# A four-layer transformer with a routed expert stage: first expert weights and output bias fetched per block, first product computed turned, gates moved to the final sum

## The chip, the cores and the metric

The kernel runs on one core of one Trainium2 chip. The metric is the device time of one execution in microseconds (us). Two executions are spoken of: the timed runs, of which there are 14, and one profiled execution, which left the trace. All durations of single instructions come from the trace.

The engines are PE (matrix products), DVE and POOL (elementwise work; POOL also issues the scatters), ACT (activation functions, which also issues some transfers) and SP, which here only issues transfers. Every engine executes its own instructions in program order.

## The reference, cut to what matters

A batch of 64 x 64 tokens of width 128 passes an attention layer with relative positions (L0), a self/cross attention layer with a feed-forward part (L1), a gating layer (L2), and a last layer (L3): self attention, cross attention and a mixture of 8 experts, of which each token uses 2. Only the last step is touched:

```
h      = layer_norm(x)
logits = h @ rw.T + rb
vals, idx = top_k(logits, 2);  gates = softmax(vals)
h1 = gelu(h @ fc1_w[e].T + fc1_b[e])          # 128 -> 512, for expert e
eo = h1 @ fc2_w[e].T + fc2_b[e]               # 512 -> 128
out = x + gates[0] * eo[idx 0] + gates[1] * eo[idx 1]
```

## The kernel before, in words

The 4096 tokens are worked on in 8 groups of 512 (4 blocks of 128 tokens, `NBLK`). The first layer has its order written out by hand. For the other layers the Python generators of `drive` (line 149) put out the instructions of several groups alternately, and a scheduler orders each engine's instructions at build time by its own model; `experts` (line 649) is the "fill" that `drive` steps on between the others. Nearly all instructions carry line 74, that of a helper, so groups are told apart by tile names.

**Routing** (`router`, line 1279, once for each group). It takes the two best experts and their gates, counts the rows of each expert with small products (`pr`), and scatters each normalised token twice, to the places of its two experts, into a table in device memory (`hrows`, POOL, 8 scatters per group). Each row carries 4 more columns: token number, first expert, and two gate values (lines 1345 to 1347). Then lines 1367 to 1379 build the matrix of gates, turn it on PE (`pgt`), copy it (DVE, `T<-pgt`), multiply it with the output biases of all experts (`tok<-fc2b`) and add the result to `x`.

**Tables** (`table`, line 657). When all groups of a part are routed (5 groups in the first part, 3 in the second, `PARTS`), DVE computes for each block of 128 rows its place in `hrows` and its expert. There are 47 and 31 blocks (`NSLOT`), 78 in all.

**Blocks** (the loop of line 822). In step t the program puts out, in this order: `load(t+6)`, `first(t)`, `hidden_turned(t-1)`, `second(t-3)`, `turn(t+2)`.

- `load` (710): SP reads the block's place out of the table into a register (`value`, a TENSOR_LOAD at line 311), computes the address, and issues the transfer of 128 rows into one of 8 places (`rin`, in the trace under the name `km`).
- `turn` (719): PE turns the rows (`xt`), ACT scales them and adds the shift (`vp`); DVE computes where each result row goes (`tob`) and its gate (`m`) in four small instructions.
- `first` (744): PE reads the expert's place into a register and multiplies: 128 tokens by 512 hidden columns, one product `f<-fcw,vp` with the tokens as stationary operand. `fcw` holds both weights of all 8 experts on chip (1024 columns for each). DVE copies the 512 columns out (`h`).
- `hidden_turned` (753): four PE transposes (`ht`), then four Gelu instructions on ACT, with the bias of the first product as per-partition scalar.
- `second` (768): four products that add up into 128 tokens by 128 columns; DVE multiplies by the gate on the way out (`y`, in the trace `km<-f,m`), and POOL scatters the result (`yrows`).

In the trace each of these fp32 products stands as two MATMUL records, a transpose as one.

**Sums** (`read` 789, `summed` 804). When all results of a part are scattered, the two result rows of each token are read back (one transfer on SP's queue, one on ACT's), POOL adds `x` and the first, DVE adds the second, and SP writes the output. For the 5 groups of the first part this goes on between the blocks of the second part; the last 3 groups are summed at the end.

The 8 transfers of first weights are issued with the 8 of second weights in `load_expert` (1409), long before the experts start.

Of the kernel before, what the change touches and what calls it, by code (L numbers as in the profile page):

```python
# [16 lines left out]
P = 128  # L17
# [16 lines left out]
ROWW = D + 4  # L34
NEG = -1.0e30
EPS = 1e-5

# [57 lines left out]
def kernel(ctx: ExitStack, tc: tile.TileContext, a: dict, out: bass.AP):  # L95
# [553 lines left out]
    def experts():  # L649
# [7 lines left out]
        def table(h):  # L657
# [11 lines left out]
            for e in range(1, NE):  # L669
# [13 lines left out]
            nc.vector.scalar_tensor_tensor(rb, eb, float(REGION), jb, op0=ALU.mult, op1=ALU.add)  # L683

            nc.vector.tensor_scalar(rb, rb, float(NE * REGION), float(P), ALU.min, ALU.mult)
            tab = wtile([1, 2, ns], f"table{h}", 1, I32)
            nc.vector.tensor_copy(tab[:, 0, :], rb[0:1, :])
            nc.vector.tensor_scalar(
                tab[:, 1, :], eb[0:1, :], float(NE - 1), 1024.0, ALU.min, ALU.mult
            )  # L690

            hot = wtile([NE, ns], "hotb", 1)
            nc.vector.tensor_scalar(hot, eb[0:NE, :], lane[0:NE, :], None, ALU.is_equal)
# [12 lines left out]
        def slot(i):  # L706
            h = sum(i >= LAST[k] for k in range(NH))
            return h, i - (LAST[h] - NSLOT[h])

        def load(i):  # L710
            h, j = slot(i)
            rows_in = rin[i % 8]
            at = value(nc.sync, tables[h][0][0:1, 0, j : j + 1], NE * REGION * P)
            ld = nc.sync.dma_start(rows_in, hrows[h][bass.ds(at, P), :])
            for sc in done["scatters"][h]:
                tc.add_manual_dep(ld.ins, sc.name, LANDED, reason="all rows are in place")
            held[i] = {"in": rows_in}

        def turn(i):
            h, j = slot(i)  # L720
            b = held[i]
            rows_in = b["in"]
            pt = pmm("xt")
            nc.tensor.transpose(pt[:, 0:P], rows_in[:, 0:D], ident)
            b["x"] = wtile([P, P], "vp", 3)
            nc.scalar.activation(b["x"], pt[:, 0:P], AF.Identity, scale=col("moe_g"), bias=col("moe_b"))

            m = wtile([P, 3], "m", 12)
            b["to"] = wtile([P, 1], "tob", 16, U32)
            nc.vector.tensor_tensor(  # L730
                m[:, 0:1], rows_in[:, D + 1 : D + 2], tables[h][1][:, j : j + 1], ALU.is_equal
            )
            nc.vector.tensor_tensor(
                m[:, 2:3], rows_in[:, D + 1 : D + 2], tables[h][1][:, j : j + 1], ALU.not_equal
            )
            nc.vector.tensor_scalar(
                b["to"], m[:, 2:3], float(PARTS[h] * T), rows_in[:, D : D + 1], ALU.mult, ALU.add
            )
            nc.vector.tensor_scalar(
                m[:, 1:2], m[:, 0:1], rows_in[:, D + 3 : D + 4], rows_in[:, D + 2 : D + 3], ALU.mult, ALU.add  # L740
            )
            b["gate"] = m[:, 1:2]

        def first(i):
            h, j = slot(i)
            b = held[i]
            b["e"] = value(nc.tensor, tables[h][0][0:1, 1, j : j + 1], (NE - 1) * 1024)
            ps = pmm("f1")
            nc.tensor.matmul(ps, lhsT=b["x"], rhs=fcw[:, bass.ds(b["e"], 512)], start=True, stop=True)
            b["u"] = wtile([P, 512], "h1", 4)  # L750
            nc.vector.tensor_copy(b["u"], ps)

        def hidden_turned(i):
            h, j = slot(i)
            b = held[i]
            pt = pmm("ht")
            for c in range(NFC):
                nc.tensor.transpose(pt[:, c * P : (c + 1) * P], b["u"][:, c * P : (c + 1) * P], ident)
            b["h"] = wtile([P, 512], "s", 10)
            for c in range(NFC):  # L760
                nc.scalar.activation(
                    b["h"][:, c * P : (c + 1) * P], pt[:, c * P : (c + 1) * P], AF.Gelu,
                    bias=tables[h][2][:, c, j : j + 1],
                )

# [2 lines left out]
        def second(i):  # L768
            h, j = slot(i)
            b = held.pop(i)  # L770
            po = pmm("f2")
            for c in range(NFC):
                nc.tensor.matmul(
                    po[:, 0:D], lhsT=b["h"][:, c * P : (c + 1) * P],
                    rhs=fcw[:, bass.ds(b["e"] + (512 + c * D), D)],
                    start=(c == 0), stop=(c == NFC - 1),
                )
# [44 lines left out]
        for t in range(-6, total + 3):  # L822
            h = sum(t + 6 >= at for at in LAST)
            while h < NH and done["routed"] < sum(PARTS[: h + 1]):
                yield
            if h < NH and h not in tables:
                yield from table(h)
            if t + 6 < total:
                load(t + 6)
            if 0 <= t < total:  # L830
                first(t)
            if 0 <= t - 1 < total:
                hidden_turned(t - 1)
            if 0 <= t - 3 < total:
                second(t - 3)
            if 0 <= t + 2 < total:
                turn(t + 2)

            for h in range(NH - 1):
                gl, at = divmod(t - 3 - LAST[h] - 4, 4)  # L840
# [15 lines left out]
    def other_layers(ends):  # L856
# [4 lines left out]
        fc2b = wtile([NE, D], "fc2b", 1)  # L861
# [4 lines left out]
        nc.scalar.dma_start(fc2b, a["fc2b"])  # L866

        bkm = wtile([P, 2, 4], "bkm", 1)
        for i, name in enumerate(("sa_in_b", "ca_in_b")):
# [409 lines left out]
        def router(g, hT, x, zx):  # L1279
# [59 lines left out]
            nc.vector.tensor_tensor(e2, e2, g1, ALU.mult)  # L1339
# [6 lines left out]
            nc.vector.tensor_copy(meta(2), e2)  # L1346
            nc.vector.tensor_tensor(meta(3), g1, e2, ALU.subtract)
            for n in range(2):
                if g < NG - 1:
                    yield  # L1350
# [14 lines left out]
            yield  # L1365

            gates = wtile([P, NBLK, NE], "gates", 3)
            nc.vector.tensor_tensor(gates, hots[0], last(g1[:, :], NE), ALU.mult)
            nc.vector.tensor_tensor(hots[1], hots[1], last(e2[:, :], NE), ALU.mult)
            nc.vector.tensor_tensor(gates, gates, hots[1], ALU.add)  # L1370
            yield
            pgt = extra("pgt")
            for k in range(NBLK):
                nc.tensor.transpose(pgt[0:NE, k * P : (k + 1) * P], gates[:, k, :], ident)
            gT = wtile([NE, T], "T", 4)
            nc.vector.tensor_copy(gT, pgt[0:NE, :])
            yield
# [26 lines left out]
        return pools["mid"].tile(shape, dtype, tag=name, name=name)  # L1404


    fcw = mtile([P, NE * 1024], "fcw")

    def load_expert(e):
        nc.scalar.dma_start(fcw[:, e * 1024 : e * 1024 + 512], a["fc1"][e])  # L1410
        nc.scalar.dma_start(
            v3(fcw[:, e * 1024 + 512 : (e + 1) * 1024], NFC), a["fc2"][e].rearrange("(f c) d -> c f d", c=P)
        )

    start = mtile([P, NE], "start")
# [85 lines left out]
```

## Time and profile before

| | us |
|---|---|
| median of the 14 timed runs (lowest to highest) | 1761.66 (1756.85 to 1767.45) |
| the profiled execution's own time | 1758.07 |
| its span in the trace | 1756.3 |
| busy: PE / DVE / ACT / POOL | 1614.6 / 1214.0 / 992.6 / 914.0 |
| first row load issued by SP | 1520.9 |
| last result scatter issued by POOL | 1740.4 |

How to read it: times in windows count from the start of the span. The slices on the page cut the span into 40 equal parts, one digit each, in tenths. In a group's or tile's line come engine, operation, operands (result, then sources), count, and duration in nanoseconds as least/median/most. Engine names with a q (SPq) are an engine's own queue of issuing and register instructions, which are not counted as busy. An arrow in square brackets says how long an engine was idle before and what ended that. The clock (PEclk) is the share of full speed that PE was granted.

### The profile page before, as it was taken

How to read it: one execution, taken by the hardware profiler on the slowest of the kernel's cores; microseconds unless marked ns; L12 is line 12 of the kernel's file. 1: busy time of each engine (PE TensorE's matmuls, PEld its weight loads, DVE VectorE, ACT ScalarE, POOL GpSimd, SP SyncE). 2: the span in 40 equal slices, each digit the busy share in tenths (PEclk: the TensorE clock that was granted, in tenths of full speed). 3: DMA queues.
4: the chain of work that ended last, by engine and by line, in shares of the span. 5: the costliest groups of instructions: out<-in, count | busy, mean ns of one | idle time of the engine just before them, and what ended most of it. 6: DMA issues, size and time to landing. Idle time of an engine off the chain costs nothing.

```text
span 1756.3 us, 46242 instructions
## 1 busy us (share of the span) xinstructions
PE 1614.6 (92%) x18026; PEld 1165.2 (66%) x18026; DVE 1214.0 (69%) x3289; ACT 992.6 (57%) x2712; POOL 914.0 (52%) x875
## 2 busy tenths in 40 slices
PE   7799999999999999699998999899888988679996
PEld 5566666666666666477676776667666767557774
DVE  4577676767676767578877786777566874556663
ACT  4456464646464645255655556666677853236663
POOL 3445464646473737567766666534222243554454
PEclk9999999999999999899999999999889987589998
DMA  6664554555455545410000000000000000112143
GB/s 175 157 162 137 134 140 130 140 130 140 129 139 132 139 140 152 150 37 8 11 26 28 26 15 13 13 2 2 8 14 14 2 21 20 55 51 57 54 122 90
DMA packets 215160, 136.78 MB, mean 78 GB/s; under 512 B 38896, under 2 KB 198786, under 8 KB 214816
## 3 DMA queue, kind: packets, MB, share of 16 engines
q1 hardware_dynamic: 186880, 90.54, 20.6%
q10 hardware_dynamic: 23520, 34.75, 6.1%
q0 software_dynamic: 4544, 8.54, 1.4%
q8 instruction: 144, 2.36, 0.6%
q14 instruction: 72, 0.59, 0.1%
HBM read 66.51 MB, written 68.19 MB: 77 GB/s over the span
## 4 chain that ended last, share of the span: by engine, by line
PE 64%; DVE 16%; ACT 8%; POOL 5%; issue 3%; DMA 3%; another core or an unknown queue 1%; POOLq 0%; SPq 0%; ACTq 0%; DVEq 0%
PE av L74 8%; PE psv L74 8%; PE proj L74 7%; PE pt L74 6%; PE psk L74 6%; PE f L74 6%; PE tok L74 5%; PE pbd L74 4%; PE psc L74 3%; DVE mx L74 3%; DVE s L74 3%; PE acc L74 3%; PE sc L74 3%; ACT z L74 3%; PE tr L74 2%
## 5 line engine op out<-in xcount | busy, mean ns | idle before, releaser
L74 ACT ACTIVATE s<-s,nm 128x128 f32<-128x128 f32 x512 | 198.0, 388 | 245.4 <-DVE nm L74 221.6
L74 POOL TENSOR_TENSOR s<-s,sm 128x512 f32<-128x512 f32 x128 | 130.6, 1042 | 257.1 <-DVE sm L74 257.1
L74 PE MATMUL pt<-ident,s 128*128 128x128 f32 x1536 | 213.4, 282 | 21.4 <-ACT kT L74 7.8
L74 POOL TENSOR_TENSOR s<-s,mx 128x512 f32<-128x512 f32 x160 | 164.1, 1046 | 110.9 <-DVE mx L74 110.7
L74 PEld LDWEIGHTS pt<-ident,s 128*128 128x128 f32 x1536 | 176.5, 145 | 42.3 <-issue 15.7
L74 ACT ACTIVATE pT<-pt 128x512 f32<-128x512 f32 x256 | 142.0, 606 | 83.0 <-PE pt L74 72.1
L74 POOL TENSOR_TENSOR rs<-rs,nhalf 128x4 f32<-128x4 f32 x80 | 81.6, 1021 | 189.6 <-DVE rs L74 157.3
L74 POOL TENSOR_TENSOR skew<-skew,mb 128x512 f32<-128x512 f32 x128 | 160.1, 1273 | 29.9 <-DMA skew<-scr 29.3
L74 PEld LDWEIGHTS av<-vb,pT 128*64 128x64 f32 x4096 | 133.0, 143 | 21.0 <-issue 16.3
L74 PE MATMUL av<-vb,pT 128*64 128x18 f32 x4096 | 141.3, 216 | 4.7 <-issue 2.5
L74 DVE TENSOR_REDUCE mx<-s 128x8 f32<-128x512 f32 x160 | 102.8, 674 | 44.2 <-ACT s L74 44.2
L74 POOL DMA_INDIRECT yrows<-km,tob x78 | 76.3, 979 | 99.2 <-DVE m L74 71.1
L74 PE MATMUL psv<-wv,kv 128*128 128x256 f32 x512 | 127.4, 392 | 0.0
L74 PE MATMUL psk<-kv,wk 128*128 128x512 f32 x256 | 127.0, 618 | 0.0
L74 PE MATMUL sc<-km,qs 32*64 32x256 f32 x2048 | 106.0, 425 | 19.6 <-ACT qs L74 13.9
L74 DVE COPY pT<-pt 128x512 f32<-128x512 f32 x128 | 82.1, 682 | 37.5 <-PE pt L74 37.5
L74 PEld LDWEIGHTS psv<-wv,kv 128*128 128x128 f32 x512 | 92.2, 189 | 15.1 <-issue 1.0
L74 PEld LDWEIGHTS av<-pT,v 128*64 128x64 f32 x2048 | 66.5, 138 | 52.8 <-issue 31.1
L74 PEld LDWEIGHTS pbd<-rT,qp 64*128 64x128 f32 x1024 | 62.1, 187 | 57.4 <-DVE qp L74 55.7
L74 DVE TENSOR_TENSOR s<-sc,mb 128x512 f32<-128x512 f32 x128 | 81.8, 680 | 26.0 <-PE sc L74 25.9
L74 DVE TENSOR_TENSOR s<-psc,skew 128x512 f32<-128x512 f32 x128 | 87.4, 683 | 13.6 <-issue 7.3
L74 ACT ACTIVATE z<-z,nmr,rs 128x128 f32<-128x128 f32 x160 | 66.2, 492 | 53.3 <-DVE nmr L74 39.5
(237 smaller groups left out, 3746.5 us busy)
## 6 DMA issues: line engine op xcount, KB each, us to landing
scr<-stage SPq DMA_DIRECT2D x64, 516.0 KB
skew<-scr SPq DMA_DIRECT2D x128, 256.0 KB
hrows<-pad ACTq DMA_DIRECT2D x66, 330.0 KB
ctx<-in_ctxT SPq DMA_DIRECT2D x24, 256.0 KB
km<-hrows SPq DMA_DIRECT2D x78, 66.0 KB
fcw<-in_fc ACTq DMA_DIRECT2D x16, 256.0 KB
kv<-in_xT SPq DMA_DIRECT2D x8, 256.0 KB
kv<-in_ctxT SPq DMA_DIRECT2D x8, 256.0 KB
```

What stands on the lines that cost most here:

```text
L74: ins = it(*args, **kw)
```

## The change

1. `fcw` keeps only the second weights. In `load`, SP reads a second table value (the expert), and issues two more transfers for each block: the first weights (128 x 512, 256 KB) into a ring of 6 (`w1s`) and the output bias of the expert, repeated to all 128 partitions (64 KB), into a ring of 8 (`b2s`). `load_expert` issues 8 transfers instead of 16.
2. `first` makes the product turned: four products, each with 128 columns of the weights as stationary operand and the block's 128 tokens streaming. The result has hidden columns on partitions, and Gelu reads it straight from PSUM; the copy `h` and the four transposes are gone, and `second` follows two steps after `first` instead of three.
3. `second` adds the bias on the way out instead of multiplying by the gate. The table `gate` keeps the two gates of each token on chip, and `summed` applies them: eight DVE instructions of 128 x 128 for each group, none on POOL.
4. The gate columns of the rows (528 to 520 bytes) and the gate computation in `turn` (four instructions to two) go, and so does the part of `router` that multiplies gates by biases.
5. In a step the program now puts out `first(t)`, `second(t-2)`, `load(t+6)`, `turn(t+2)`.

```diff
@@ table
-            tab = wtile([1, 2, ns], f"table{h}", 1, I32)
+            tab = wtile([1, 3, ns], f"table{h}", 1, I32)
...
+            nc.vector.tensor_scalar(tab[:, 2, :], eb[0:1, :], float(NE - 1), None, ALU.min)
@@ load
+            w, bias = w1s[i % 6], b2s[i % 8]
+            e = value(nc.sync, tables[h][0][0:1, 2, j : j + 1], NE - 1)
+            nc.sync.dma_start(w, a["fc1"][bass.ds(e, 1), :, :].rearrange("o p f -> (o p) f"))
+            nc.sync.dma_start(bias, a["fc2b"][bass.ds(e, 1), :].to_broadcast([P, D]))
@@ first
-            nc.tensor.matmul(ps, lhsT=b["x"], rhs=fcw[:, bass.ds(b["e"], 512)], start=True, stop=True)
-            b["u"] = wtile([P, 512], "h1", 4)
-            nc.vector.tensor_copy(b["u"], ps)
-        def hidden_turned(i):
...
-                nc.tensor.transpose(pt[:, c * P : (c + 1) * P], b["u"][:, c * P : (c + 1) * P], ident)
+                nc.tensor.matmul(
+                    ps[:, c * P : (c + 1) * P], lhsT=b["w"][:, c * P : (c + 1) * P], rhs=b["x"],
+                    start=True, stop=True,
+                )
@@ second
-            nc.vector.tensor_scalar(y, po[:, 0:D], b["gate"], None, ALU.mult)
+            nc.vector.tensor_tensor(y, po[:, 0:D], b["bias"], ALU.add)
@@ summed
-            nc.gpsimd.tensor_tensor(o, ys[0], v3(xs[g][:, :], NBLK), ALU.add)
-            nc.vector.tensor_tensor(o, o, ys[1], ALU.add)
+            for k in range(NBLK):
+                nc.vector.scalar_tensor_tensor(
+                    o[:, k, :], ys[0][:, k, :], gate[:, g, 0, k : k + 1], x3[:, k, :], op0=ALU.mult, op1=ALU.add
+                )
+                nc.vector.scalar_tensor_tensor(
+                    o[:, k, :], ys[1][:, k, :], gate[:, g, 1, k : k + 1], o[:, k, :], op0=ALU.mult, op1=ALU.add
+                )
@@ the loop of steps
-            if t + 6 < total:
-                load(t + 6)
             if 0 <= t < total:
                 first(t)
-            if 0 <= t - 1 < total:
-                hidden_turned(t - 1)
-            if 0 <= t - 3 < total:
-                second(t - 3)
+            if 0 <= t - 2 < total:
+                second(t - 2)
+            if t + 6 < total:
+                load(t + 6)
@@ router, at the end
-            gates = wtile([P, NBLK, NE], "gates", 3)
...
-            pb = tokens_by(lambda c: gT, lambda c: fc2b)
-            nc.vector.tensor_tensor(x, pb, x, ALU.add)
@@ load_expert
-        nc.scalar.dma_start(fcw[:, e * 1024 : e * 1024 + 512], a["fc1"][e])
```

More of the change, by code (lines that the diff above doesn't have):

```diff
@@ L33 @@
 LAST = [sum(NSLOT[: h + 1]) for h in range(NH)]
-ROWW = D + 4
+ROWW = D + 2
 NEG = -1.0e30
@@ L685, in table @@
             nc.vector.tensor_scalar(rb, rb, float(NE * REGION), float(P), ALU.min, ALU.mult)
-            tab = wtile([1, 2, ns], f"table{h}", 1, I32)
+            tab = wtile([1, 3, ns], f"table{h}", 1, I32)
             nc.vector.tensor_copy(tab[:, 0, :], rb[0:1, :])
             nc.vector.tensor_scalar(
-                tab[:, 1, :], eb[0:1, :], float(NE - 1), 1024.0, ALU.min, ALU.mult
+                tab[:, 1, :], eb[0:1, :], float(NE - 1), 512.0, ALU.min, ALU.mult
             )
+            nc.vector.tensor_scalar(tab[:, 2, :], eb[0:1, :], float(NE - 1), None, ALU.min)
             hot = wtile([NE, ns], "hotb", 1)
@@ L716, in load @@
                 tc.add_manual_dep(ld.ins, sc.name, LANDED, reason="all rows are in place")
-            held[i] = {"in": rows_in}
+            w, bias = w1s[i % 6], b2s[i % 8]
+            e = value(nc.sync, tables[h][0][0:1, 2, j : j + 1], NE - 1)
+            nc.sync.dma_start(w, a["fc1"][bass.ds(e, 1), :, :].rearrange("o p f -> (o p) f"))
+            nc.sync.dma_start(bias, a["fc2b"][bass.ds(e, 1), :].to_broadcast([P, D]))
+            held[i] = {"in": rows_in, "w": w, "bias": bias}
         def turn(i):
@@ L726, in turn @@
             nc.scalar.activation(b["x"], pt[:, 0:P], AF.Identity, scale=col("moe_g"), bias=col("moe_b"))
-            m = wtile([P, 3], "m", 12)
+            m = wtile([P, 1], "m", 12)
             b["to"] = wtile([P, 1], "tob", 16, U32)
-            nc.vector.tensor_tensor(
-                m[:, 0:1], rows_in[:, D + 1 : D + 2], tables[h][1][:, j : j + 1], ALU.is_equal
-            )
[L733 to L742, printed above, removed]
+            nc.vector.tensor_scalar(
+                m, rows_in[:, D + 1 : D + 2], tables[h][1][:, j : j + 1], float(PARTS[h] * T),
+                ALU.not_equal, ALU.mult,
+            )
+            nc.vector.tensor_tensor(b["to"], m, rows_in[:, D : D + 1], ALU.add)
         def first(i):
@@ L746, in first @@
             b = held[i]
-            b["e"] = value(nc.tensor, tables[h][0][0:1, 1, j : j + 1], (NE - 1) * 1024)
+            b["e"] = value(nc.tensor, tables[h][0][0:1, 1, j : j + 1], (NE - 1) * 512)
             ps = pmm("f1")
-            nc.tensor.matmul(ps, lhsT=b["x"], rhs=fcw[:, bass.ds(b["e"], 512)], start=True, stop=True)
-            b["u"] = wtile([P, 512], "h1", 4)
-            nc.vector.tensor_copy(b["u"], ps)
-        def hidden_turned(i):
-            h, j = slot(i)
-            b = held[i]
-            pt = pmm("ht")
             for c in range(NFC):
-                nc.tensor.transpose(pt[:, c * P : (c + 1) * P], b["u"][:, c * P : (c + 1) * P], ident)
+                nc.tensor.matmul(
+                    ps[:, c * P : (c + 1) * P], lhsT=b["w"][:, c * P : (c + 1) * P], rhs=b["x"],
+                    start=True, stop=True,
+                )
             b["h"] = wtile([P, 512], "s", 10)
@@ L761, in hidden_turned @@
                 nc.scalar.activation(
-                    b["h"][:, c * P : (c + 1) * P], pt[:, c * P : (c + 1) * P], AF.Gelu,
+                    b["h"][:, c * P : (c + 1) * P], ps[:, c * P : (c + 1) * P], AF.Gelu,
                     bias=tables[h][2][:, c, j : j + 1],
@@ L774, in second @@
                     po[:, 0:D], lhsT=b["h"][:, c * P : (c + 1) * P],
-                    rhs=fcw[:, bass.ds(b["e"] + (512 + c * D), D)],
+                    rhs=fcw[:, bass.ds(b["e"] + c * D, D)],
                     start=(c == 0), stop=(c == NFC - 1),
@@ L806, in summed @@
             o = wtile([P, NBLK, D], "o", 2)
-            nc.gpsimd.tensor_tensor(o, ys[0], v3(xs[g][:, :], NBLK), ALU.add)
-            nc.vector.tensor_tensor(o, o, ys[1], ALU.add)
+            x3 = v3(xs[g][:, :], NBLK)
+            for k in range(NBLK):
[5 more added lines that the diff above has]
+                )
             nc.sync.dma_start(out[g * NBLK : (g + 1) * NBLK].rearrange("k p d -> p k d"), o)
@@ L821, in experts @@
         reads = {}
-        for t in range(-6, total + 3):
+        for t in range(-6, total + 2):
             h = sum(t + 6 >= at for at in LAST)
@@ L827, in experts @@
                 yield from table(h)
+            if 0 <= t < total:
+                first(t)
+            if 0 <= t - 2 < total:
+                second(t - 2)
             if t + 6 < total:
                 load(t + 6)
-            if 0 <= t < total:
-                first(t)
-            if 0 <= t - 1 < total:
-                hidden_turned(t - 1)
-            if 0 <= t - 3 < total:
-                second(t - 3)
             if 0 <= t + 2 < total:
@@ L839, in experts @@
             for h in range(NH - 1):
-                gl, at = divmod(t - 3 - LAST[h] - 4, 4)
+                gl, at = divmod(t - 2 - LAST[h] - 4, 4)
                 if 0 <= gl < PARTS[h]:
@@ L860, in other_layers @@
         rw = wtile([P, NE], "rw", 1)
-        fc2b = wtile([NE, D], "fc2b", 1)
         nc.scalar.dma_start(w2l, a["w2l"])
@@ L865, in other_layers @@
         nc.scalar.dma_start(rw, a["rw"])
-        nc.scalar.dma_start(fc2b, a["fc2b"])
         bkm = wtile([P, 2, 4], "bkm", 1)
@@ L1338, in router @@
             nc.vector.reciprocal(g1, g1)
-            nc.vector.tensor_tensor(e2, e2, g1, ALU.mult)
+            nc.vector.tensor_copy(gate[:, g, 0, :], g1)
+            nc.vector.tensor_tensor(gate[:, g, 1, :], e2, g1, ALU.mult)
             def meta(c):
@@ L1345, in router @@
             nc.vector.tensor_copy(meta(0), tok[:, PLACE[g][1] * NBLK : (PLACE[g][1] + 1) * NBLK])
-            nc.vector.tensor_copy(meta(2), e2)
-            nc.vector.tensor_tensor(meta(3), g1, e2, ALU.subtract)
             for n in range(2):
@@ L1364, in router @@
             done["routed"] += 1
-            yield
-            gates = wtile([P, NBLK, NE], "gates", 3)
[L1368 to L1377, printed above, removed]
-            pb = tokens_by(lambda c: gT, lambda c: fc2b)
-            nc.vector.tensor_tensor(x, pb, x, ALU.add)
         fb = cols[:, _C["fc1_b"][0] : _C["fc1_b"][1]].rearrange("p (e c) -> p c e", c=NFC)
@@ L1404, in mtile @@
         return pools["mid"].tile(shape, dtype, tag=name, name=name)
-    fcw = mtile([P, NE * 1024], "fcw")
+    fcw = mtile([P, NE * 512], "fcw")
+    w1s = [mtile([P, 512], f"w1s{i}") for i in range(6)]
+    b2s = [mtile([P, D], f"b2s{i}") for i in range(8)]
+    gate = mtile([P, NG, 2, NBLK], "gate")
     def load_expert(e):
-        nc.scalar.dma_start(fcw[:, e * 1024 : e * 1024 + 512], a["fc1"][e])
         nc.scalar.dma_start(
-            v3(fcw[:, e * 1024 + 512 : (e + 1) * 1024], NFC), a["fc2"][e].rearrange("(f c) d -> c f d", c=P)
+            v3(fcw[:, e * 512 : (e + 1) * 512], NFC), a["fc2"][e].rearrange("(f c) d -> c f d", c=P)
         )
```

## The prediction, as put on record before the run

> **What bounds the kernel now.** I read the page's slices first, then the busy times by window, then PE's timeline inside a window, then SP's queue there. The page:
>
> ```profile
> span 1756.3 us, 46242 instructions
> PE   7799999999999999699998999899888988679996
> PEclk9999999999999999899999999999889987589998
> ```
>
> (PEclk is the clock that PE was granted.) Everything that the change touches lies in the last eighth, apart from the loads of the weights near 730 us. The windows there (window, its length, busy PE, PEld, DVE, ACT, POOL with counts, clock, DMA share, GB/s):
>
> ```profile
> 1500.00:1550.00 50.00, 33.42 (x143) 23.58 (x142) 27.40 (x187) 11.40 (x31) 28.62 (x30) 0.64 0.20 59
> 1577.00:1681.00 104.00, 104.00 (x680) 80.22 (x679) 71.66 (x264) 66.23 (x219) 42.39 (x44) 1.00 0.24 65
> ```
>
> Until 1575 no engine is full: the last groups' routing, POOL's scatters and the first blocks wait for each other. From 1577 PE is busy all of 104 us and nothing else is. One period of PE's timeline (start, length, operation):
>
> ```profile
> 1657.84 0.27 PE L74 MATMUL xt<-ident,km 128*128 128x128 f32 x1
> 1657.95 1.02 PE L74 MATMUL f<-fcw,vp 128*128 x2
> 1658.81 0.60 PE L74 MATMUL ht<-ident,h 128*128 128x128 f32 x4
> 1659.25 1.06 PE L74 MATMUL f<-fcw,s 128*128 x8
> 1660.14 0.27 PE L74 MATMUL xt<-ident,km 128*128 128x128 f32 x1
> ```
>
> Lengths overlap; starts count. One block: xt 0.11, first product 0.86, transposes 0.44, second product 0.89, together 2.30 us. The second product shows the price of a record with 128 streaming columns and its own weights: 0.89/8 = 0.111.
>
> SP is the queue that the change loads. Five row loads that ran nearly unhindered, their register loads, and SP's waits in the stretch from 1576 to 1680 (total, times, longest):
>
> ```profile
> L74 SPq DMA_DIRECT2D km<-hrows x5: 332/332/333, 1529.9 to 1533.4; - x5
> L311 SPq TENSOR_LOAD <-table x5: 267/268/272, 1530.2 to 1533.8; - x5
> SPq L74 <- PE xt L74: 57.9, 43, 2.8
> ```
>
> Five issues lie 3.5 us apart from first to last: 3.5/4 = 0.88 us for each load, of which 0.33 is the transfer's issue, 0.27 the register load, 0.28 address, semaphores and gaps. In the full stretch SP waited 57.9 of 104 us, so 46.1/45 blocks = 1.02 us at most went to a load.
>
> **The change, part by part.**
>
> *PE, per block.* The product turned is 4 x 2 records of 128 columns: 8 x 0.111 = 0.89 in place of 0.86. The transposes' 0.44 go. New sum 0.11 + 0.89 + 0.89 = **1.89**, 0.41 less. The first product's weights now change with each record, but so they do in `f<-fcw,s`, whose cadence I used.
>
> *DVE, ACT, POOL, per block.* DVE loses the copy `h` (0.69) and two of four small instructions; adding the bias costs what the gate's product did (0.35). ACT keeps four Gelu and `vp`: 66.23 us in 45 blocks, 1.47 each. POOL keeps one scatter per block, at 1.27 when back to back. None reaches 1.89; this gains nothing by itself.
>
> *SP, per block.* Before: one load, 0.88. After: rows 0.88, weights with their own register load 0.88, bias without one, 0.88 - 0.27 - 0.05 = 0.56. Sum **2.32 us**, more than PE's 1.89 and level with the old 2.30. The issue itself depends little on size (ctx, 256 KB in rows of 2 KB: median 328 ns; rows: 332). Bounds: 2.2 if semaphore waits share a slot; 2 x 1.02 + 0.70 = 2.74 if the full stretch's 1.02 is all work. I take 2.32, since the five loads had the fewest waits in them.
>
> A rule speaks against the change here. The Trainium skill, "DMA: Bandwidth & Descriptors", section "Latency and other measured facts", puts a floor of about 600 ns under a tensor_load. The rows here show 268. By the page a block would cost SP 2 x 0.33 more, 2.98 us, and the sum below would end some 50 us later; the measured row decides.
>
> *Waits added.* The weights' transfer waits for `first` six blocks back, the bias for DVE's add eight back. Behind them in SP's queue stand the next rows, read-backs and output writes; PE's `xt` waits for the rows. With SP slowest these waits are over before SP arrives.
>
> *Data.* 320 KB more per block. In the crowded window 727 to 750 the engines moved 231 GB/s; in the full stretch they are 24% busy at 65 GB/s. At 2.32 us per block the addition is 138 GB/s, total about 200: carried, with latency. Lower bound 0; upper bound, if issues slow to the 445 ns of fcw's loads in that crowd, 3 x 0.11 = 0.33 per block. That end lies inside the 2.74.
>
> *Sums.* POOL's add (1.26) and DVE's (0.69) become eight DVE instructions. No such row exists; a 128 x 512 add takes 0.69, so a quarter with its fixed part about 0.22; a 128 x 128 `z` on chip took 0.16 to 0.35. I take 0.28, 2.2 per group. SP's output write waits for it: read-back issued, 3 us to land, 2.2 to sum, against 4.6 us of SP's other work in between: about 1 us lost, five times; plus ten issues of 0.45. Together **9** (4 to 15).
>
> *Routing.* Eight groups lose 4 `pgt`, 8 `tok<-fc2b`, a copy and an add. Mostly they fill waits, but at the start of the experts two are on the path: DVE, with the table half made, waits for such a product,
>
> ```profile
> 1510.15 0.69 DVE L74 TENSOR_TENSOR x<-tok,x 128x512 f32<-128x512 f32 x1 [2.67 <-PE tok L74]
> ```
>
> and it delays the turning of the last group's rows. I take 2.5 earlier for SP's first load (0 to 5).
>
> *Eight fewer weight loads near 730.* The chain there runs over POOL and PE, not over these transfers; 0 (-2 to 0). Rows of 520 bytes: 0.
>
> *The sum.* SP starts at 1520.9 - 2.5 = 1518.4. Its work is 78 x 2.32 = 181. Before, it lost time in the crowded start: loads 1 to 6 took 8.6 us for 4.4, and all engines stood from 1549.2 to 1560.6; I keep 15 (4 to 25, since I have no cause for these gaps). With 9 for the sums the last weights go out at 1723. Landing 2 (rows issued at 1520.9 were used at 1522.6), first 0.9, Gelu 0.5, second 0.9, add and gap 0.9: last scatter at about **1728.5**, before 1740.4. The end: the last output waits as before for the first one's buffer, two sums of 2.2 for 1.95: +0.5. Net -11.4. The profiled execution's 1758.07 becomes 1746.7; it lay 3.6 under the median of 1761.66, so against the median I say **1750**.
>
> If SP were not slowest, PE would be late next; if SP's cover for PE's gain goes, nothing else hides 0.41 x 78 = 32 us.
>
> **Rivals.**
>
> *A: PE stays the bound.* SP is ahead by six blocks and stays so. From block 11 (1577.2) 66 x 1.89 puts the last first product at 1702 instead of 1733.5: -31.5, and -2.4 for the shorter pipeline, -2.5 start, +0.5 end: -36, 1726. For it: SP idled over half of the stretch. Against: two issues and a register load more per block; SP would need under 1.89. Chance 0.08.
>
> *B: SP's pace makes it slower.* One mechanism, SP's issue path, in its steady pace of 45 to 70 blocks. It decides at 2.32 + 11.4/78 = 2.47 us per block. For it: the 1.02 of the full stretch, and these four loads, 2.1 us apart, in which single register instructions took 700 ns while POOL scattered:
>
> ```profile
> L74 SPq DMA_DIRECT2D km<-hrows x4: 4/14/700, 1523.0 to 1529.4; - x4
> ```
>
> Against: no such thing in the quiet stretch. At 2.6 it is +22 - 11.4, 1772. Chance 0.30.
>
> *C: gain and loss cancel* (SP at 2.42 to 2.49, or the start no earlier): within 1758 to 1765. Chance 0.12.
>
> PE would be 81% busy under my forecast, with gaps. In 1500 to 1550 it was 67% busy at a clock of 0.64; in the full stretch it held 1.00. At 0.8 it would need 2.36 per block, 3 us in all, which the range holds. The Trainium skill, "TensorE: Matmul & The Clock Gate", section "What's actually happening", has only half and full speed, and half after an idle window of about 3.4 us; by that, gaps of 0.4 us would not trip it and the 3 us would be 0. No row here shows PE at 81% in such short gaps.
>
> **How the numbers follow.** My forecast 0.50, A 0.08, C 0.12, B 0.30. Some 2 in 50 of the first end within 0.2% (about what a measurement can tell from no change). Faster: 0.08 + 0.46 = 0.54; same 0.12 + 0.03 = 0.15; slower 0.31. The forecast's own range is 1738 to 1758 (start and sums). The range 1736 to 1774 leaves out A and the upper end of B (2.74).
>
> **What would show it.** Right: row loads in the trace 2.3 to 2.4 us apart with SP waiting for little, and PE idle before `xt` or the first product, released by a DMA. PE's records at 0.111 and no `ht`. Last scatter near 1728. Wrong: SP waiting for PE (A), issues well over 333 ns or pace above 2.47 (B), DVE's sums idle for their read-backs longer than 3 us, or a first block later than 1530.

## The result, and the profile after

The changed kernel is **slower**, by 1.2%: 1782.68 us (median of 6 runs, 1779.31 to 1785.72) against 1761.24 for the kernel before (28 runs, 1754.84 to 1769.22), a ratio of 1.012 with the 95% interval 1.0105 to 1.0135. In two later groups of runs it was 1.0112 (1.0089 to 1.0135) and 1.0092 (1.0067 to 1.0117). The profiled execution took 1785.03, its span is 1783.2.

The page after, the same slices as before with the DMA share added:

```profile
span 1783.2 us, 46715 instructions
...
PE   7799999999999999699999999898989987478874
...
PEclk9999999999999999899999998899889875589997
DMA  6765555555455555300001000000000000267775
```

PE's last eight slices went from 88679996 to 87478874, and the DMA engines, which were a quarter busy in the even stretch before, now show 7 tenths. The windows after (columns as in the prediction), once in the even stretch and once where sums are made between the blocks:

```profile
1606.00:1661.00 55.00, 47.26 (x384) 44.54 (x385) 13.81 (x69) 35.42 (x112) 22.47 (x23) 1.00 0.73 191
1682.00:1755.00 73.00, 53.17 (x407) 48.87 (x407) 22.35 (x104) 36.81 (x124) 22.50 (x23) 0.97 0.73 199
```

PE was busy 104 of 104 us; now it is busy 86% and 73%, and no other engine is full. 23 row loads in 55 us are 2.39 us for each block, 25 in the 75.0 us from load 52 to load 77 are 3.0. Who is late? PE's timeline in the even stretch, and the one wait of any length that PE has there (total, times, longest):

```profile
1636.35 1.06 PE L74 MATMUL f<-vp,w1s 128*128 128x128 f32 x8
1637.25 1.06 PE L74 MATMUL f<-fcw,s 128*128 x8
1638.14 0.27 PE L74 MATMUL xt<-ident,km 128*128 128x128 f32 x1
1638.25 1.06 PE L74 MATMUL f<-vp,w1s 128*128 128x128 f32 x8
```
```profile
PE xt L74 <- DMA km<-hrows: 6.8, 8, 1.5
```

Starts count: 0.90, 0.89, 0.11. When PE works without waiting, a block takes it 1.90, and what it waits for is the row load. SP's own queue in the same microseconds (only transfers are listed; register loads and addresses fill the rest):

```profile
1637.55 0.30 SPq L74 DMA_DIRECT2D km<-hrows  x1
1638.40 0.33 SPq L74 DMA_DIRECT2D w1s<-in_fc  x1
1638.98 0.33 SPq L74 DMA_DIRECT2D b2s<-in_fc2b  x1
1639.84 0.33 SPq L74 DMA_DIRECT2D km<-hrows  x1
```

From rows to rows 2.29: 0.85, 0.58, 0.86. SP never rests in this. In the whole window its waits for others add up to 1.7 us of 55. SP between blocks 52 and 77, where it also issues read-backs (`s<-yrows`) and output writes:

```profile
1719.42 0.33 SPq L74 DMA_DIRECT2D b2s<-in_fc2b  x1
1720.77 0.40 SPq L74 DMA_DIRECT2D out<-o  x1
1721.67 0.33 SPq L74 DMA_DIRECT2D km<-hrows  x1
1723.23 0.00 SPq L74 DMA_DIRECT2D w1s<-in_fc  x1
```

The output write cost 1.4 us from the issue before it (it waits for DVE's sum), and the weights behind it came 1.56 after the rows instead of 0.85.

**Where the 26.9 us between the two spans lie.** I use the start of a block's second product, read from the two traces:

| | before | after | difference |
|---|---|---|---|
| last product of the first layer (not touched) | 719.5 | 722.9 | 3.4 |
| from there to block 10's second product | 865.0 | 865.2 | 0.2 |
| block 10 to block 77 (67 blocks) | 153.4 | 175.0 | 21.6 |
| block 77 to the end | 18.4 | 20.1 | 1.7 |

Pace holds 21.6 of the 26.9: 2.29 us per block before, 2.61 after. 3.4 lie in the first layer, which the change does not touch, and 1.7 at the end. SP's first row load came 17.3 us later (1538.2 instead of 1520.9), and yet block 10 came at the same time in both.

### The profile page after: what moved, and what is told of

The parts are those of the page before. It is cut to its first block, busy times and chain, and to the rows that moved or that the text cites. A ratio compares the mean times of both kernels' runs of the same rounds, so it can differ in the third digit from the quotient of the medians.

```text
span 1783.2 us, 46715 instructions
## 1 busy us (share of the span) xinstructions
PE 1589.7 (89%) x18086; PEld 1178.8 (66%) x18086; DVE 1139.3 (64%) x3065; ACT 995.0 (56%) x2712; POOL 903.3 (51%) x867
## 5 line engine op out<-in xcount | busy, mean ns | idle before, releaser
L74 DVE TENSOR_TENSOR s<-sc,mb 128x512 f32<-128x512 f32 x128 | 81.8, 679 | 23.2 <-PE sc L74 23.2
```

The lines of the kernel that those rows point to most:

```text
L74: ins = it(*args, **kw)
```

## The experiments

**Theory 1**, after the two traces: SP's issues set the pace. **Rival 2**: the bytes do, 385 KB per block. **Rival 3**: the transfers in SP's queue make the late start, and that is the loss. The groups of runs were made on different chips. The kernel before, which ran beside every group, took 1738.55 and 1740.67 us in two of the groups and 1761.24, 1766.06 and 1771.89 in the others; I call the first kind the short machine and the other the long machine. So only ratios to the kernel before of the same group, and paces, are compared. The changed kernel ran on long machines only. The two versions that ran on both kinds have ratios up to 0.004 apart, so a ratio from a short machine set beside the changed kernel's is an estimate, good to about that. "Pace" is block 10 to block 77, per block.

| run | ratio to the kernel before (95%) | pace | machine |
|---|---|---|---|
| kernel before (first profile, again) | 0.9998 (0.9984 to 1.0011) | 2.29, 2.29 | long |
| changed (first, again, third) | 1.012, 1.0112, 1.0092 | 2.61, 2.63, 2.65 | long |
| bias on chip, again | 0.9838 (0.9822 to 0.9855), 0.9838 (0.9817 to 0.9859) | 2.05, 2.06 | short |
| one transfer for both | 0.9856 (0.983 to 0.9881) | 2.12 | short |
| half the weights | 1.0079 (1.0049 to 1.0108) | 2.58 | long |
| bias twice | 1.0601 (1.0583 to 1.0618) | 3.68 | short |
| product not turned | 1.0072 (1.0048 to 1.0096) | 2.58 | short |
| sums off SP | 1.0074 (1.0054 to 1.0095) | 2.55 | long |
| gates only, again | 0.997 (0.9958 to 0.9981), 0.9947 (0.9924 to 0.9969) | 2.27, 2.28 | short, long |
| copy on chip, again | 0.9775 (0.9759 to 0.9792), 0.9812 (0.9775 to 0.9849) | 1.96, 1.99 | short, long |
| later scatters | 1.0113 (1.008 to 1.0146) | 2.71 | long |

### Taking the bias out of SP's queue

```diff
-            nc.sync.dma_start(bias, a["fc2b"][bass.ds(e, 1), :].to_broadcast([P, D]))
...
+            ev = value(nc.vector, tables[h][0][0:1, 3, j : j + 1], (NE - 1) * D)
+            nc.vector.tensor_tensor(y, po[:, 0:D], ball[:, bass.ds(ev, D)], ALU.add)
```

> The changed kernel, but the output bias of all experts is put on chip once (one transfer at the start of the experts) and the add on DVE picks its expert's row by a register; SP keeps the rows and the first weights of each block. Theory 1 (SP's issues set the pace of the changed kernel, 2.3 to 2.4 us per block of which the bias is 0.56, and the late start of the experts comes from the moved gates): SP needs 1.8 per block, PE at 1.89 takes over; 78 x 0.5 = 39 us less than the changed kernel's 1783, so 1738 to 1752, with the first row load still near 1538. Rival 2 (the transfers' data set the pace, 384 KB per block at 190 GB/s): only 64 of 390 KB go, pace 2.0 to 2.1, 1755 to 1762. Rival 3 (the per-block transfers in SP's queue also make the late start): the first row load comes earlier by 6 us or more.

> The version with the bias on chip once more, for a comparison with the others on one chip: 1.4 to 1.8% under the kernel before, and within 0.5% of the version with one transfer for weights and bias.

1710.05 and 1712.58 us, both 0.9838 of the kernel before: faster than it, and, by the ratios, some 2.8% under the changed kernel. (The 1738 to 1752 us expected were reckoned from the changed kernel's 1783 on a long machine; these two groups ran on short ones.) PE is full again:

```profile
1560.00:1615.00 55.00, 55.00 (x493) 54.79 (x492) 16.09 (x88) 43.29 (x144) 29.29 (x30) 1.00 0.72 205
```

Without this one issue of 64 KB the pace fell by 0.56 per block (2.61 to 2.05). That this is the very sum forecast for its SP instructions is partly luck: SP now needs about 2 x 0.88 = 1.76, PE's 1.89 is the bound again (1.94 per block from block 10 to block 52), and so PE ends the gain. The first row load came at 1516.1, so it did come earlier than in the changed kernel, but on the other machine: no verdict on rival 3 from here.

### The same bytes with one issue less, and fewer bytes with the same issues

One transfer brings weights and bias, laid side by side in memory:

```diff
-        "fc1": L3["e_fc1_w"].transpose(0, 2, 1), "fc2": L3["e_fc2_w"].transpose(0, 2, 1),
+        "fc1": np.concatenate(
+            [L3["e_fc1_w"].transpose(0, 2, 1), np.broadcast_to(L3["e_fc2_b"][:, None, :], (NE, P, D))], axis=2
+        ),
...
-            nc.sync.dma_start(bias, a["fc2b"][bass.ds(e, 1), :].to_broadcast([P, D]))
+            held[i] = {"in": rows_in, "w": w, "bias": w[:, 512 : 512 + D]}
```

> The changed kernel with the output bias laid behind the first weights in memory (128 x 640 per expert, the bias repeated in every row), so that one transfer brings both: the bytes of the changed kernel, 385 KB per block, with one issue less. Theory 1 (number of issues): SP's pace falls by 0.56 to about 1.8 and PE's 1.89 takes over, with the read-backs and output writes still on SP some 2.5 in blocks 52 to 77; 2.4 to 3.0% under the changed kernel, 1.2 to 1.8% under the kernel before, as with the bias on chip. Rival 2 (data): as the changed kernel, 1.0 to 1.2% over the kernel before.

The ring of weights has 8 places here instead of 6. The other way round, half of the weights with all issues (the half is used twice, so the results are not the reference's):

```diff
-            nc.sync.dma_start(w, a["fc1"][bass.ds(e, 1), :, :].rearrange("o p f -> (o p) f"))
+            nc.sync.dma_start(w[:, 0 : 2 * P], a["fc1"][bass.ds(e, 1), :, 0 : 2 * P].rearrange("o p f -> (o p) f"))
...
-                    ps[:, c * P : (c + 1) * P], lhsT=b["w"][:, c * P : (c + 1) * P], rhs=b["x"],
+                    ps[:, c * P : (c + 1) * P], lhsT=b["w"][:, c % 2 * P : (c % 2 + 1) * P], rhs=b["x"],
```

> The changed kernel, but each block transfers only the first half of its expert's first weights (128 KB in place of 256) and uses it twice, so the output is not the reference's. The number of SP's instructions is the same. Theory 1 (SP's issues): no change, within 0.3% of the changed kernel on this chip. Rival 2 (data): 262 in place of 390 KB per block, pace down to 1.9 (PE then), 25 to 35 us less.

The windows, first of one transfer, then of half the weights (the last two columns are DMA share and GB/s):

```profile
1560.00:1615.00 55.00, 55.00 (x493) 54.84 (x492) 15.95 (x85) 43.12 (x142) 29.89 (x31) 1.00 0.84 244
```
```profile
1606.00:1661.00 55.00, 46.65 (x375) 43.40 (x374) 13.29 (x67) 34.47 (x109) 21.49 (x22) 1.00 0.49 129
```

One transfer for both took 1715.43 us, within 0.2% of the bias on chip on the same machine. With an issue less the DMA engines carry 244 GB/s and PE is full; with a third of the bytes less they carry 129 and PE idles as much as in the changed kernel. The time of the second was 4.9 us (0.3%) under the changed kernel's in the same group, where rival 2 asked for 25 to 35. Rival 2 falls: it is the number of issues. The two more places in the ring do not explain the gain: in the changed kernel's even stretch SP's waits ended by PE's products, those for a place among them, were 1.0 us of 55. The Trainium skill, "Perfetto Trace Analysis", section "DMA Instruction — HWDGE (DVE, Sync)", says that the record of such a transfer on its issuing engine covers a wait for a lock, the making of descriptors and the semaphore, and not the movement of data; the runs agree, 333 ns in the median for 256 KB of weights as for 65 KB of rows.

### One issue more

```diff
+            nc.sync.dma_start(b3s[i % 8], a["fc2b"][bass.ds(e, 1), :].to_broadcast([P, D]))
```

> The changed kernel with the bias transfer of each block issued a second time into a spare ring that nothing reads. Theory 1 (SP's issues): one more issue of 0.56 per block, without a register load, so the pace goes from 2.4 to 2.95 and the time up by 78 x 0.56 = 44 us, to 1820 to 1830. Rival 2 (data): 64 KB more at 190 GB/s, 0.34 per block, 26 us, 1805 to 1812. If neither SP nor data sets the pace: 1783.

1842.02 us, by estimate about 84 over the changed kernel (taken as 1757.7, 1.011 times the kernel before of that group). The direction is theory 1's, the size is twice its: 1.07 per block, not 0.56. The queue shows why (first fence: SP's issues; second: SP's longest kind of wait between 1576 and 1700; third: median us from issue to landing):

```profile
1622.45 0.33 SPq L74 DMA_DIRECT2D b2s<-in_fc2b  x1
1623.86 0.33 SPq L74 DMA_DIRECT2D km<-in_fc2b  x1
1624.85 0.33 SPq L74 DMA_DIRECT2D km<-hrows  x1
```
```profile
SPq L74 <- DMA km<-in_fc2b: 12.3, 17, 1.2
```
```profile
km<-in_fc2b SPq DMA_DIRECT2D x78, 64.0 KB, 7.1
```

The second bias goes out 1.41 after the first, not 0.56. In the records of this program eight semaphores take turns on the transfers that SP and ACT issue, and each issue first waits on the semaphore that it will use, until the transfer that used it last has landed. With four transfers per block that one is two blocks back: 2 x 3.68 = 7.4 us, and landing takes 7.1. So SP's queue has a second limit here, eight transfers in flight. SP's waits that a landing ended add up to 15.4 us from 1576 to 1700, 0.46 for each of the 33.7 blocks; that is most of the 0.51 by which 1.07 exceeds 0.56.

Does this limit hold the changed kernel back as well? With three transfers per block, eight reach 2.67 blocks back, 7.0 us at its pace. Its own trace has no landing times, but the version whose product is not turned (next section) has the same three transfers per block, nearly the same pace (2.58), and nearly all landings in its trace. SP's waits there that a landing ended, from block 10 to block 77 (the bias goes by the name `km<-in_fc2b`):

```profile
SPq L74 <- DMA pT<-yrows: 4.3, 1, 4.3
SPq L74 <- DMA w1s<-in_fc: 0.5, 1, 0.5
SPq L74 <- DMA km<-in_fc2b: 0.2, 1, 0.2
```

0.7 us in 173 for the blocks' transfers, and one longer wait for a read-back: with three transfers per block the limit hardly bites.

### What the turned product is worth

```diff
-                    ps[:, c * P : (c + 1) * P], lhsT=b["w"][:, c * P : (c + 1) * P], rhs=b["x"],
...
+            nc.tensor.matmul(ps, lhsT=b["x"], rhs=b["w"], start=True, stop=True)
+            b["u"] = wtile([P, 512], "h1", 4)
+            nc.vector.tensor_copy(b["u"], ps)
...
+                nc.tensor.transpose(pt[:, c * P : (c + 1) * P], b["u"][:, c * P : (c + 1) * P], ident)
```

> The changed kernel with the first product computed as before (rows times weights, copied by DVE, transposed by PE), but with the weights from the ring and the bias transferred for each block; everything else as changed. PE then needs 2.30 per block in place of 1.89. Theory 1 (SP's 2.5 to 2.6 is the pace of the changed kernel): PE's 0.41 is hidden under SP, the time is within 0.4% of the changed kernel (1.0 to 1.6% over the kernel before). If PE's turned product had been a part of what sets the changed kernel's pace: 10 us or more slower than the changed kernel, 1.8% over the kernel before or more.

1754.14 us, 1.0072. That is below the 1.0 to 1.6% over the kernel before that theory 1 expected, and nowhere near the 1.8% of its rival; but this is a short machine, so it doesn't show that this version is faster than the changed kernel. The even stretch (columns as before):

```profile
1600.00:1655.00 55.00, 53.72 (x349) 41.15 (x348) 28.31 (x93) 34.13 (x112) 21.93 (x24) 1.00 0.76 187
```

PE does 2.30 of work per block instead of 1.89 and hides it (53.72 us busy of 55); the pace is 2.58, against 2.61 to 2.65 for the changed kernel. While SP is the bound, the product's new form buys nothing.

### The sums off SP

```diff
-                ld = (nc.sync, nc.scalar)[k].dma_start(
+                ld = nc.scalar.dma_start(
...
-            nc.sync.dma_start(out[g * NBLK : (g + 1) * NBLK].rearrange("k p d -> p k d"), o)
+            nc.gpsimd.dma_start(out[g * NBLK : (g + 1) * NBLK].rearrange("k p d -> p k d"), o)
```

> The changed kernel with the read-backs and the output writes of the sums taken from SP's queue: both read-backs from ACT's, the output write from POOL's. Theory 1: in blocks 53 to 77 the pace was 3.0 us, because SP, which has no slack, stood for the read-back's scatters and for each finished sum; without them it is 2.4 there, 15 us less in the blocks, of which the end may take back up to 5: 10 to 15 us under the changed kernel. If something else (ACT, DVE's eight instructions per sum, DMA) sets the 3.0: within 4 us.

1778.42, 8.5 us under the changed kernel of the same group (1786.85). From block 52 to 77 the second products came 2.42 apart instead of 2.62, 5 us, less than the 15 expected. SP's waits for others between loads 52 and 77 went from 9.6 to 6.3 us. So read-backs and outputs on SP's queue explain only a part of the slow end. The rest of the 8.5 lies elsewhere: in the profiled executions block 10 came 857.8 us after the first layer's end, 7.2 earlier than in the changed kernel, and no run shows why.

### The moved gates alone, and the late start

All weights and biases on chip, old product, gates at the sum:

> The kernel before with one part of the change alone: the gates are applied when a token's results are summed, the routing loses its gate products and the folded bias, and the bias (on chip for all experts) is added by DVE as each block's second product is evicted. First weights on chip, first product as before. Theory 1: the late start comes from this part, so the first row load is near 1535 instead of 1521; the pace is PE's 2.30 as before, and the sums cost 3 to 9 us; 1770 to 1785. Rival 3 (the transfers make the late start): first row load at 1516 to 1524, 1758 to 1768. Rival 4 (the late start varies from execution to execution): times scatter by over 10 us.

> The kernel with the moved gates alone once more, for its start on the other chip. If that chip is the one with the long kernel before: theory 5 puts the first row load at 1530 to 1540 with the moved gates alone, as in the changed kernel, since the routing's order on the engines is the same; its time then goes from 0.3% under the kernel before to 0.2 to 0.8% over it. Rival 3 (the transfers): first load at 1521 to 1527 as in the kernel before, time 0.3% under. On the same chip as then: 0.3% under the kernel before, again.

0.997 and 0.9947: this part is a small gain, 6 and 11 us, where theories 1 and 5 expected a loss. And its start answers rival 3: on the long machine the first row load came at 1540.9, as late as in the changed kernel, with no transfers of weights or bias; on the short one at 1515.1. Here are the same DVE instructions of the same program, first on the long machine, then on the short one (start, length, what; in brackets the idle time before):

```profile
1530.67 0.42 DVE L74 TENSOR_SCALAR table<-eb 1x47 int32<-1x47 f32 x1
1531.27 0.21 DVE L74 TENSOR_TENSOR pT<-index,pT 128x47 f32<-128x47 f32 x1 [0.18 <-DVE table L74]
1532.67 0.23 DVE L74 TENSOR_TENSOR cand<-cand,desc 128x32 f32<-128x32 f32 x1 [1.19 <-DVE pT L74]
...
1534.80 0.19 DVE L74 TENSOR_REDUCE ci<-cand 128x4 f32<-128x32 f32 x1 [1.75 <-remote]
```
```profile
1511.98 0.17 DVE L74 TENSOR_SCALAR table<-eb 1x47 int32<-1x47 f32 x1
1512.07 0.19 DVE L74 TENSOR_TENSOR pT<-index,pT 128x47 f32<-128x47 f32 x1
1512.19 0.17 DVE L74 TENSOR_TENSOR cand<-cand,desc 128x32 f32<-128x32 f32 x1
...
1512.44 0.17 DVE L74 TENSOR_REDUCE ci<-cand 128x4 f32<-128x32 f32 x1
```

From the first of these starts to the last, 4.1 us on the long machine and 0.46 on the short one, while POOL issues row scatters back to back, about 1.27 apart, on both. **Theory 5**: on the long machine a burst of scatters slows the others, and the new order puts the table into such a burst. So I held the last three groups' scatters back until the table is done:

```diff
+                    if g >= PARTS[0]:
+                        tc.add_manual_dep(sc.ins, done["table"], LANDED, reason="the table first")
```

> The changed kernel with one wait more: the row scatters of the last three groups (routed rows of the second half) wait on POOL until DVE has finished the first half's block table. Theory 5 (on the chip with the long kernel before, 1761 to 1766 us, the other engines get about one instruction through per scatter while POOL issues row scatters back to back, and in the changed kernel the table lies wholly in such a burst): the burst ends with the first half's last row, the table takes 2 us again, and the first row load comes 8 to 12 us earlier than in the changed kernel (near 1528 to 1530 on that chip); time down by 5 to 12 us, since the burst, and with it some of the slowing, is only moved. Rival 6 (the slow stretch has nothing to do with POOL's burst): first load as late as before, time unchanged or later. On the other chip (kernel before at 1738): no effect, within 0.2%.

The table came 10 us earlier, the first row load at 1531.1 (counted from the first layer's end, 805.4 instead of 815.3). And then the burst caught SP instead:

```profile
1536.73 0.69 SPq L74 DMA_DIRECT2D b2s<-in_fc2b  x1
1540.28 0.01 SPq L74 DMA_DIRECT2D km<-hrows  x1
1543.90 0.70 SPq L74 DMA_DIRECT2D w1s<-in_fc  x1
1548.09 0.71 SPq L74 DMA_DIRECT2D b2s<-in_fc2b  x1
```

Issues 4 us apart, loads 0 to 10 in 48.0 us instead of 38; 1794.5 us, 5.3 over the changed kernel of the same group. Theory 5's first half held: the slow part moved with the burst. Most of SP's instructions of about 0.7 us lie between 1548.6 and 1567.1 in the changed kernel of the same group, whose last burst runs from 1545.1 to 1564.0, and between 1533.9 and 1562.1 here, with the burst from 1530.3 to 1559.4. Its 5 to 12 us did not come: the changed kernel had put out three row loads before the burst began, this version none, and load 10 came at the same point in both (853.1 and 853.4 us after the first layer's end). The earlier first load ran into the burst and was worth nothing.

### Weights copied on chip, and the two kernels again

```diff
-            nc.sync.dma_start(w, a["fc1"][bass.ds(e, 1), :, :].rearrange("o p f -> (o p) f"))
...
+            ew = value(nc.vector, tables[h][0][0:1, 1, j : j + 1], (NE - 1) * 1024)
+            nc.vector.tensor_copy(b["w"], fcw[:, bass.ds(ew, 512)])
```

No transfers per block but the rows; DVE copies the weights to a fixed place (0.43 us in the median).

> The changed kernel without its per-block transfers: all weights and biases on chip, and DVE copies an expert's first weights (128 x 512) into a fixed tile for each block, so that the product can be computed turned. Theory 1: SP is at 0.9 to 1.0 per block, PE's 1.89 is the bound, or DVE if copy (0.35 to 0.7) and two register loads bring it there; with the first row load still near 1536, 78 x 1.89 = 147 us and 10 to 15 lost in the crowded start, the last scatter is near 1710 and the end near 1727 (1715 to 1740). Rival 3: first row load near 1520, the end near 1710. If PE's turned product costs more than 0.111 a record (its weights change with each), the pace stays at 2.1 or more: 1745 and later.

> The version that copies the first weights on chip, once more. If its lead of 2.2% over the kernel before holds on the other chip too, it is 1718 to 1735 there (theory 5: its start may lose up to 12 us); on the same chip 1699.

1698.82 and 1738.41 us: 2.2% and 1.9% under the kernel before, **the fastest version**. PE is full (55.00 of 55 us from 1560 to 1615), DVE busy 34.73. The pace of 1.96 to 1.99 is PE's 1.89 and a little; against the gates alone on the same machines the turned product gained 33.8 and 22.9 us. (The first time is below the expected range, which was reckoned for a late start; the second is 3 us above its own.)

> The changed kernel as it is, beside the kernel before, on a chip on which the kernel before is profiled as well. In the four runs above the first row load lay at 1514 to 1516 whichever part of the change was in them, so theory 1 gives up the moved gates as the cause of the late start: on a chip that shows no slow stretches after 1480 the first load should lie near 1516, the pace at 2.3 to 2.4 us, and the time at 0.4 to 0.8% over the kernel before, all of it from SP's pace and its waits in blocks 53 to 77. Rival 3 (rows, weights and bias together make the late start): first load at 1530 or later again.

> The changed kernel on whatever chip this call gets. On the chip with the short kernel before (1738): first row load at 1514 to 1517, loads 0 to 10 in 24 to 28 us, 10 to 52 in 104, 52 to 77 in 74, last scatter near 1731, so 1747 to 1752, 0.4 to 0.8% over the kernel before. On the other: 1.1 to 1.2% over, again.

> The kernel before, profiled on this chip as the reference for the start. If the slow stretches between 1480 and 1565 belong to the chip or the execution and not to the kernel, this profile is some 20 us shorter than the first one, with the whole difference after 1447 us. Its time is the kernel before's within 0.2%.

All three fell on the long machine: 1786.85, 1789.23 and 1764.38 us. The changed kernel was 1.1% and 0.9% over the kernel before. Its first load was late both times (1542.4, 1540.5), against the first of these expectations; block 10's second product came 865.0 and 864.5 us after the first layer's end, and 865.9 in the kernel before. The kernel before did not get shorter, so the slow stretch belongs to this kind of machine, not to one execution.

## Why the prediction was wrong, step by step

It said 1750, faster, with B (SP's pace makes it slower, 1772) at 0.30. B's mechanism is what happened, SP's issues setting the pace; the late start came on top of it. Two steps failed: the start ("SP starts at 1520.9 - 2.5 = 1518.4") and SP's price for a block, with its waits put at nothing.

- **PE's 1.89 per block**: right, 1.90 between starts; no `ht`, and records at 0.111.
- **SP becomes the bound**: right, by the runs with an issue less, with an issue more, with fewer bytes and with more work on PE. Its 2.32 was the pace of an undisturbed cycle (2.29 above; loads 34 to 40 at 2.32). The step "I take 2.32, since the five loads had the fewest waits in them" failed as a mean: from load 10 to load 52 it was 2.47 (103.7 us where 97.4 were forecast). The median distance between two row loads there was 2.34; eight of the 42 distances, those over 2.6, hold 5.2 of the 6.3 us of difference. That 2.47 is the point from which B decides, as the prediction had it.
- **Sums, 9 (4 to 15)**: their own price was right, what they do to the others was missing. The nine read-backs and output writes between load 52 and load 77 lengthened SP's queue by 8.3 us (from the issue before to the issue after, less 0.86). The eight DVE instructions of a sum took 2.2 us together, as forecast: 346 ns each, but a start every 0.26. Yet load 52 to 77 took 75.0 where 58 + 9 were forecast. "With SP slowest these waits are over before SP arrives" failed here. SP's longest waits and DVE's waits for a read-back, between 1682 and 1755:

```profile
SPq L74 <- DMA pT<-yrows: 3.2, 2, 2.2
SPq L74 <- DVE m L74: 2.6, 2, 1.4
SPq L74 <- DVE tob L74: 2.0, 2, 1.1
```
```profile
DVE o L74 <- DMA s<-yrows: 13.5, 5, 3.2
```

All of SP's waits there add up to 11.4 us, and SP has no work in hand to make up for them. DVE executes in program order: it stands up to 3.2 us for a read-back to land (one of the prediction's signs of being wrong), then sums for 2.2, and the blocks' instructions (`m`, `tob`, `km`) that set SP's places free stand behind it. That these waits, and not something else, make the 8 us too many is argued from the trace; no run moved the sums off DVE.

- **The start**: the step that turned the sign. "SP starts at 1520.9 - 2.5 = 1518.4" put load 10 at 1556.6 and with it block 10's second product more than 20 us ahead of the kernel before's 1584.5. My own sum had the remaining 67 blocks 11 us *slower* (164.4 against 153.4); all of the forecast gain was this head start. The first load came at 1538.2, 19.8 later, 3.4 of that from the first layer. The 15 lost in the crowded start fitted, by luck, since it had no cause: loads 0 to 10 took 38.0 us where 23.2 + 15 were forecast. So load 10 came at 1576.2, 3.4 of the difference from the first layer, 16.2 from the start. The row I used, an idle DVE before `tok`, was real, but without that wait the first load came no earlier: on a long machine the moved gates alone had it at 1540.9. There DVE and SP are slow while POOL issues its bursts, from a cause that stays open. On a short machine the start was as forecast (first load at 1519.5 in the version whose product is not turned), and that version was 0.7% slower than the kernel before all the same.
- **Last weights to last scatter, 5.5**: 10.5. The second product is put out two steps after the first, and landing took longer than the 2 us forecast: 5.8 to 7.1 in the median for the transfers of the run with the bias twice. This trace has no landing times, so how the 5 us divide is not shown.
- In sum, for the last scatter: 3.4 + 16.2 + 14.3 + 3.9 = 37.8 us after the forecast 1728.5, at 1766.3.
- **Data carried at 200 GB/s, cost 0**: right (191, and 244 with PE full). **tensor_load at 268 ns**: right, 268 in the median. By the 600 of the Trainium skill ("DMA: Bandwidth & Descriptors", "Latency and other measured facts") a block would, by estimate, have taken near 3 us in the even stretch, where it took 2.39. **PE's clock**: 1.00 at 86% busy with short gaps, so the 3 us set aside were 0. PE's longest wait in that stretch was 1.5 us. The rule of the Trainium skill that an idle window of about 3.4 us halves the clock ("TensorE: Matmul & The Clock Gate", "What's actually happening") agrees.
- **A** had SP ahead of PE; that is the kernel with the bias on chip, not this one.

Open: what slows the engines during POOL's burst on one kind of machine and not on the other; and what puts block 10 at the same time in both kernels on the long machine, though SP's first load is 14 to 17 us later in one of them.

## What to carry to other kernels

A queue that only issues transfers is an engine with a price per instruction: count its issues, register loads and waits per block before moving a resident operand into it, and compare with the bound that you are lowering. A wait on a queue that has become the bound has nothing to hide under, so take waiting instructions off it, or merge transfers (here 2.61 to 2.12 us per block). When a forecast gain hangs on an earlier start, ask what ended the start before, and check that the steady part alone gains.

## What the runs showed of the hardware that was not expected

- The cost of one more transfer on a queue isn't constant: 0.56 us per block for the third (without it PE is the bound, so its whole price may be more), 1.07 for a fourth, when landing (7.1 us) reached the eight transfers that this program keeps in flight. The Trainium skill, "DMA: Bandwidth & Descriptors", section "Issuing engines are not separate DMA queues", calls the sequencer's time to start a transfer usually small beside the transfer; here 0.58 to 0.88 us of the queue per transfer, register load and address included, set the pace, at 73% busy DMA engines.
- The same program (the moved gates alone) took 1732.62 us on one machine and 1761.26 on the other. Of the 31.4 us between the two profiled spans 25.3 lie between the first layer's end and block 10. There, during back-to-back scatters, DVE needed 4.1 us for a stretch of small instructions that takes 0.46 on the other machine, and in another version on a long machine SP's issues came 4 us apart.
